# Two layers of each expert as seven block products instead of eight, with streamed weights

## The chip, the cores and the metric

The kernel runs on one core of a Trainium2 chip. The core has five engines with a queue each, worked off in order: TensorE (PE, matmul; its weight loads are shown as PEld), VectorE (DVE), ScalarE (ACT), GpSimd (POOL) and SyncE (SP, which here issues nearly all DMA transfers). They wait for each other by semaphores. The metric is the device time of one execution in microseconds. SBUF is the on-chip memory that all engines read; PSUM is the small one that only PE's products go to, in eight banks of 128 x 512 fp32.

## The reference

Input is `x` of shape (1, 32, 128, 256): 4096 tokens of 256 channels. All arithmetic is fp32. There are two layers.

- Layer 0 normalises the tokens, projects q, k, v, computes masked attention over all 4096 tokens in 8 heads, and adds the projected result to its input.
- Layer 1 adds an attention in a narrow window of 24 tokens, and then a mixture of eight experts in which every expert sees every token. With `x` the normalised tokens and `w` the softmax of the router's scores:

```python
w = jax.nn.softmax(feat @ Wr + br, axis=-1)
h = jnp.einsum('bfd,edh->bfeh', x, W1) + b1
h = jax.nn.relu(_bn(h, g1, be1, m1, v1))
h = jnp.einsum('bfeh,ehk->bfek', h, W2) + b2
h = jax.nn.relu(_bn(h, g2, be2, m2, v2))
y = jnp.einsum('bfeh,ehd->bfed', h, Wo) + bo
return jnp.einsum('bfed,fe->bfd', y, w)
```

The two batch norms are per-channel scales and shifts with stored statistics, so each of the first two layers of an expert is a 256 x 256 matrix product, a scale, a shift and a relu; the last layer is a 256 x 256 product, weighted by `w` and summed over the experts.

## The kernel before

`fast_kernel` has two stages. The first, up to about 749 us, is layer 0's attention; the change touches nothing in it. The second is layer 1. Its 4096 tokens are eight blocks of 512, and each block goes through the eight experts: the list `work` has 64 pairs (block, expert). The tokens stay in SBUF, one tile of 128 x 256 for 128 tokens. For a block, `expert_tokens` normalises and `turn_tokens` transposes them into `xfT` (256 channels as two halves of 128 partitions, by 512 tokens).

`layer` (L1803 on; products on L1810, relu on L1815) computes one of the first two layers for one block and one expert. For each half `m` of the output channels it takes a PSUM bank and makes two matmuls of 512 columns, one for each half `c` of the input channels; then ACT applies scale, shift and relu to the bank in one instruction. `combine` (products on L1829, DVE on L1837) takes the last layer: eight matmuls of 256 columns into two banks of the pool `ps_y`, after which DVE multiplies by the router's weight and adds onto the tokens; after the last expert of a block the tokens are stored (L1842).

All weights of all experts lie in SBUF: `load_expert` (L1499) loads them in 24 transfers of 256 KB, most of them from `load_rest` between 761 and 790 us. PSUM banks are three for the layers (`ps_h`), two for `ps_y`, three for the other work (`ps_x`, taken with `bank`).

The order of work is the order of the program; the framework adds the semaphores and does not reorder. The main loop at the end of `fast_kernel` does, for each pair, the second layer, `insert()`, the first layer of the next pair, `insert()`, the last layer, `insert()`. So there are three job places per pair. `insert` takes up to four jobs from a list whose order, needs and costs (in us of PE) are given: the rest of layer 1 for later blocks, such as `project` (the projection of layer 0), `normalise` and `turn` (L1588, L1599), `key`, `logits` (L1620), `exponentials` (L1647), `turn_weights` (L1658), `apply` (L1669), `route` (L1732), `turn_route` (L1742), `output_biases` (L1778). A job is taken only when its needs were met in an earlier place, and a job with a cost only while the sum spent stays under a line that grows evenly until ten places before the block begins. `normalise` also issues small transfers (16 KB, L1592 and L1594) that carry edge rows to the neighbours.

A side computation (`bound_squares` and what follows it, on POOL, PE and ACT) bounds the scores and decides on a flag whether a general version must run as well; with these inputs it does not.

In the framework, two accesses to the same PSUM bank of one tile are kept in program order, one of them a write; in SBUF the regions themselves are compared.

Of the kernel before, what the change touches and what calls it, by code (L numbers as in the profile page):

```python
# [16 lines left out]
P = 128  # L17
# [806 lines left out]
def fast_kernel(ctx: ExitStack, tc: tile.TileContext, ins: dict, out: bass.AP, narrow):  # L824
# [91 lines left out]
    with ExitStack() as l0:  # L916
# [540 lines left out]
    wf = ctx.enter_context(tc.tile_pool(name="wf", bufs=1))  # L1457
    W = {
        name: wf.tile([P, E, 2, D], F32, name=f"{name}_sb") for name in ("W1", "W2", "Wo")
    }  # L1460
# [16 lines left out]
    spare = {"tags": itertools.cycle("hxyhxyhx")}  # L1477
# [3 lines left out]
    def open_banks():  # L1481
        nonlocal ps_h, ps_y, ps_x
        early.clear()
        scores_ps.close()
        ps_h = ctx.enter_context(tc.tile_pool(name="ps_h", bufs=3, space=PSUM))
        ps_y = ctx.enter_context(tc.tile_pool(name="ps_y", bufs=2, space=PSUM))
        ps_x = ctx.enter_context(tc.tile_pool(name="ps_x", bufs=3, space=PSUM))
# [9 lines left out]
    def load_expert(e):  # L1497
        for name in ("W1", "W2", "Wo"):
            nc.sync.dma_start(  # L1499
                out=W[name][:, e],  # L1500
                in_=ins[f"L1_ffn_{name}"][e].rearrange("(c p) h -> p c h", p=P),
            )
# [16 lines left out]
    load_expert(0)  # L1519

    def load_rest():
        load_expert(1)
        for b in range(TPB + 1, NBLK):
            load_tokens(b, res.tile([P, TPB, D], F32, name=f"tokens{b}"))
            load_expert(b - 3)
        for e in range(NBLK - 3, E):
            load_expert(e)
        for n in range(TPB * TPB, NTILE):
            with_bias(n)
# [195 lines left out]

    def route(b):
# [56 lines left out]
    def layer_halves(src, name, l, b, e, parts=2):  # L1783

        pss = [ps_h.tile([P, BLK], F32, tag="h", name=f"psh{l}_{b}_{e}_{m}") for m in range(2)]
        for part in range(parts):
            cols = slice(part * BLK // parts, (part + 1) * BLK // parts)
            for m in range(2):
                for c in range(2):
                    nc.tensor.matmul(  # L1790
                        pss[m][:, cols], lhsT=W[name][:, e, c, m * P : (m + 1) * P],
                        rhs=src[:, c, cols], start=(c == 0), stop=(c == 1),
                    )
            if part < parts - 1:
                yield
        dst = fh.tile([P, 2, BLK], F32, tag=f"h{l}", name=f"h{l}_{b}_{e}")
        k = l * E + e
        for m in range(2):
            nc.scalar.activation(
                dst[:, m, :], pss[m], AF.Relu,  # L1800
                bias=bshift[:, m, k : k + 1], scale=bscale[:, m, k : k + 1],
            )
        yield dst  # L1803

    def layer(src, name, l, b, e):
        dst = fh.tile([P, 2, BLK], F32, tag=f"h{l}", name=f"h{l}_{b}_{e}")
        for m in range(2):
            ps = ps_h.tile([P, BLK], F32, tag="h", name=f"psh{l}_{b}_{e}_{m}")
            for c in range(2):
                nc.tensor.matmul(  # L1810
                    ps, lhsT=W[name][:, e, c, m * P : (m + 1) * P], rhs=src[:, c, :],
                    start=(c == 0), stop=(c == 1),
                )
            k = l * E + e
            nc.scalar.activation(  # L1815
                dst[:, m, :], ps, AF.Relu,
                bias=bshift[:, m, k : k + 1], scale=bscale[:, m, k : k + 1],
            )
        return dst

    def combine(ht, b, e):
        w = blk[b]["w"]
        dst = out[0].rearrange("n t d -> (n t) d")
        for r2 in range(TPB // 2):
            ps = ps_y.tile([P, 2, D], F32, tag="y", name=f"psy{b}_{e}_{r2}")
            for k in range(2):
                r = 2 * r2 + k
                for c in range(2):
                    nc.tensor.matmul(  # L1829
                        ps[:, k, :], lhsT=ht[:, c, r * P : (r + 1) * P],  # L1830
                        rhs=W["Wo"][:, e, c, :],
                        start=(c == 0), stop=(c == 1),
                    )
            for k in range(2):
                n = b * TPB + 2 * r2 + k
                r = 2 * r2 + k
                nc.vector.scalar_tensor_tensor(  # L1837
                    out=tokens(n), in0=ps[:, k, :], scalar=w[:, r, e : e + 1],
                    in1=tokens(n), op0=ALU.mult, op1=ALU.add,
                )  # L1840
                if e == E - 1:
                    nc.sync.dma_start(out=dst[n * P : (n + 1) * P], in_=tokens(n))  # L1842
# [11 lines left out]
    def bound_squares(name):  # L1854
        squares[name] = small([P, 2, D], f"sq_{name}")
# [184 lines left out]
    a = layer_halves(blk[0]["xfT"], "W1", 0, 0, 0)  # L2040
# [26 lines left out]
    for b in range(1, NBLK):  # L2067
# [33 lines left out]
        for r2 in range(TPB // 2):  # L2101
# [3 lines left out]
            )  # L2105
        job(("route", b), 0.55, lambda b=b: route(b), ("xfT", b, 0), ("xfT", b, 1))
# [9 lines left out]
        if b == 1:  # L2116
            for name in bound_of:
                job(("square", name), 0, lambda name=name: bound_squares(name))
# [18 lines left out]
    work = [(b, e) for b in range(NBLK) for e in range(E)]  # L2137
# [45 lines left out]
    for k, (b, e) in enumerate(work):  # L2183
        ht = layer(a, "W2", 1, b, e)
        insert()
        if k + 1 < len(work):
            nb, ne = work[k + 1]
            a = layer(blk[nb]["xfT"], "W1", 0, nb, ne)
        insert()
        combine(ht, b, e)  # L2190
        insert()
@with_exitstack
# [46 lines left out]
```

## Time and profile before

| | us |
|---|---|
| median of three runs (lowest to highest) | 1597.08 (1594.83 to 1597.59) |
| the profiled execution | 1596.38 |
| its span, first to last instruction | 1594.4 |
| PE busy, whole span | 1535.3 |
| DVE busy | 888.4 |
| ACT busy | 870.7 |
| POOL busy | 106.8 |
| DMA moved | 30.51 MB |

The page of the profile gives for each engine the busy time and its share, then the chain of work that ended last, followed back from the end. A group line reads: source line, engine, operation, what is written and read, shapes, count, then busy time in all and the mean duration of one in ns, then the idle time of that engine ahead of it and what ended most of that. Matmuls are pipelined: the mean duration of one is longer than the distance from one to the next, so distances are taken from start to start in the timeline. A timeline line reads: start, length of the group, engine, line, operation, count, and in brackets the idle time before it. Busy times by stretch have, after the length, busy time and count of PE, PEld, DVE, ACT and POOL, the granted clock of PE as a share of full, the DMA share and GB/s. One fp32 matmul appears as two records, which the prediction calls passes.

The mean granted clock over the span is 0.988; from 850 to 1450 us it is 1.00 and PE is busy for all but 0.2 us.

### The profile page before, as it was taken

The numbers are of one execution on the slowest core, as the hardware profiler recorded it, in microseconds if no ns is written. First come the engines' busy times: TensorE is split into PE (matmuls) and PEld (weight loads), VectorE is DVE, ScalarE is ACT, GpSimd is POOL, SyncE is SP. The second block draws the span as 40 slices with busy tenths as digits, with TensorE's granted clock in tenths as the row PEclk, the third lists the DMA queues.
The fourth block names the chain that finished last, engine by engine and source line by source line (L and its number), as shares of the span: only waits on it lengthen the run. The fifth ranks groups of instructions, "written<-read, shape, count | busy, mean of one in ns | idle before, by whom it ended". The sixth has DMA issues, their size and how long they took to land.

```text
span 1594.4 us, 20904 instructions
## 1 busy us (share of the span) xinstructions
PE 1535.3 (96%) x8171; PEld 710.3 (45%) x8171; DVE 888.4 (56%) x1508; ACT 870.7 (55%) x1156; POOL 106.8 (7%) x295
## 2 busy tenths in 40 slices
PE   8899899999999999998799999999999999999998
PEld 5333232232222222222456565566665666556555
DVE  3666778888898898999533232333332323233211
ACT  3676777878888888986243334334333342434222
POOL 1111002000000000003401000000000000000000
PEclk9999999999999999999799999999999999999999
DMA  4210000000000010000600000000000000000000
GB/s 107 60 29 17 22 8 24 8 21 8 2 8 8 1 47 21 1 8 21 203 4 1 4 14 3 14 1 10 7 4 14 0 4 14 3 14 0 14 0 15
DMA packets 36344, 30.51 MB, mean 19 GB/s; under 512 B 10008, under 2 KB 34319, under 8 KB 36239
## 3 DMA queue, kind: packets, MB, share of 16 engines
q1 hardware_dynamic: 35088, 28.02, 6.2%
q8 instruction: 66, 1.08, 0.3%
q10 hardware_dynamic: 1150, 1.09, 0.3%
q14 instruction: 40, 0.32, 0.1%
HBM read 23.63 MB, written 4.32 MB: 18 GB/s over the span
## 4 chain that ended last, share of the span: by engine, by line
PE 88%; ACT 4%; DVE 2%; DMA 2%; issue 2%; SPq 0%; POOL 0%; ACTq 0%; DVEq 0%; POOLq 0%
PE psh L1810 28%; PE sa L1248 16%; PE av L1292 14%; PE psy L1829 14%; PE psq L983 2%; ACT pt L1262 2%; PE psv L998 2%; PE psk L970 2%; PE psk L1608 2%; PE sb L1248 1%; PE sums L1318 1%; ACT pt L1260 1%; PE pso L1559 1%; PE pss L1620 1%; DVE acc L1282 1%
## 5 line engine op out<-in xcount | busy, mean ns | idle before, releaser
L1282 DVE TENSOR_TENSOR acc<-acc,pt 128x1024 f32<-128x1024 f32 (+3 forms) x500 | 525.2, 1115 | 43.8 <-ACT pt L1262 31.7
L1815 ACT ACTIVATE h<-psh,bshift,bscale 128x512 f32<-128x512 f32 x254 | 197.3, 777 | 416.9 <-PE psh L1810 416.7
L1262 ACT ACTIVATE pt<-sb 128x1536 f32<-128x1536 f32 (+3 forms) x288 | 387.3, 1345 | 3.3 <-PE sb L1248 3.2
L1248 PE MATMUL sa<-q,kT 32*128 32x512 f32 (+3 forms) x576 | 302.2, 604 | 7.3 <-ACT pt L1260 5.3
L1248 PE MATMUL sb<-q,kT 32*128 32x512 f32 (+3 forms) x1728 | 306.1, 604 | 2.2 <-ACT pt L1262 1.1
L1292 PE MATMUL av<-pt,v 128*32 128x512 f32 (+3 forms) x2304 | 286.2, 569 | 2.7 <-POOL pt L1266 1.3
L1837 DVE SCALAR_TENSOR_TENSOR tokens<-psy,w,tokens 128x256 f32<-128x256 f32 x256 | 111.8, 478 | 259.0 <-PE psy L1829 259.0
L1829 PE MATMUL psy<-Wo_sb,h 128*128 128x256 f32 x1024 | 233.3, 381 | 0.4 <-ACT h L1815 0.4
L1810 PE MATMUL psh<-h,W_sb 128*128 128x512 f32 x512 | 231.4, 595 | 0.0
L1810 PE MATMUL psh<-xfT,W_sb 128*128 128x512 f32 x504 | 227.2, 593 | 0.0
L1260 ACT ACTIVATE pt<-sa 128x512 f32<-128x512 f32 (+3 forms) x288 | 162.5, 564 | 95.0 <-PE sb L1248 70.9
L1829 PEld LDWEIGHTS psy<-Wo_sb,h 128*128 128x128 f32 x1024 | 192.1, 190 | 40.1 <-issue 15.6
L1248 PEld LDWEIGHTS sa<-q,kT 32*128 32x128 f32 x576 | 84.2, 182 | 217.5 <-ACT pt L1260 178.1
L1810 PEld LDWEIGHTS psh<-xfT,W_sb 128*128 128x128 f32 x504 | 93.4, 190 | 104.4 <-issue 102.3
L1810 PEld LDWEIGHTS psh<-h,W_sb 128*128 128x128 f32 x512 | 95.2, 190 | 99.9 <-issue 97.6
L1292 PEld LDWEIGHTS av<-pt,v 128*32 128x32 f32 x2304 | 45.4, 108 | 201.8 <-issue 182.8
L1266 POOL MEMSET pt<- 32x128 f32 (+2 forms) x192 | 58.5, 304 | 658.6 <-ACT pt L1262 574.3
L1248 PEld LDWEIGHTS sb<-q,kT 32*128 32x128 f32 x1728 | 88.0, 182 | 9.5 <-ACT pt L1262 6.9
L1282 DVE TENSOR_TENSOR acc<-pt,pt 128x1024 f32<-128x1024 f32 (+1 forms) x32 | 36.7, 1188 | 35.5 <-ACT pt L1262 30.6
L1635 DVE SCALAR_TENSOR_TENSOR s<-pss,negb,bandb 128x144 f32<-128x144 f32 x64 | 16.1, 294 | 47.4 <-PE pss L1620 47.4
L1679 DVE SCALAR_TENSOR_TENSOR tokens<-psa,sum,tokens 128x256 f32<-128x256 f32 x32 | 15.0, 468 | 44.9 <-PE psa L1673 44.9
L1745 POOL MEMSET w<- 128x128 f32 x8 | 1.6, 206 | 533.5 <-DVE tokens L1837 533.5
(227 smaller groups left out, 959.0 us busy)
## 6 DMA issues: line engine op xcount, KB each, us to landing
xg<-in_x_dram SPq DMA_DIRECT2D x32, 128.0 KB
tokens<-in_x_dram SPq DMA_DIRECT2D x8, 512.0 KB
W_sb<-in_L_ffn_W_dram SPq DMA_DIRECT2D x16, 256.0 KB
out_dram<-tokens SPq DMA_DIRECT2D x32, 128.0 KB
rec<-flat SPq DMA_DIRECT2D x60, 64.0 KB
xs<-in_x_dram SPq DMA_DIRECT2D x24, 128.0 KB
Wo_sb<-in_L_ffn_Wo_dram SPq DMA_DIRECT2D x8, 256.0 KB
xh<-xl SPq DMA_DIRECT2D x62, 16.0 KB
```

The source lines that it names most:

```text
L970: nc.tensor.matmul(ps, lhsT=wKT[:, c, g * P : (g + 1) * P], rhs=hT[:, c, :], start=(c == 0), stop=(c == 1),)
L983: nc.tensor.matmul(ps, lhsT=wcT[:, c, g * P : (g + 1) * P], rhs=hT[:, c, :], start=(c == 0), stop=(c == 1),)
L1248: nc.tensor.matmul((sb[:, h - 1, :] if h else sa)[:, lo:], lhsT=kT[rows, g, j * P : (j + 1) * P], rhs=q[rows, g, lo:], start=True, stop=True,)
L1260: nc.scalar.activation(pt[:, 0, lo:], sa[:, lo:], AF.Exp, scale=SCALE)
L1262: nc.scalar.activation(pt[:, 1:, lo:], sb[:, :, lo:], AF.Exp, scale=SCALE)
L1266: nc.gpsimd.memset(pt[k * N : (k + 1) * N, :, lo : lo + k * N], 0.0)
L1282: nc.vector.tensor_tensor(live[b, g][:, hs, lo:], old[:, hs, lo:], pt[:, hs, lo:], op=ALU.add)
L1292: nc.tensor.matmul(av[h * HD : (h + 1) * HD, lo:], lhsT=v[:, j, (g * HG + h) * HD : (g * HG + h + 1) * HD], rhs=pt[:, h, lo:], start=(j == ...
L1810: nc.tensor.matmul(ps, lhsT=W[name][:, e, c, m * P : (m + 1) * P], rhs=src[:, c, :], start=(c == 0), stop=(c == 1),)
L1815: nc.scalar.activation(dst[:, m, :], ps, AF.Relu, bias=bshift[:, m, k : k + 1], scale=bscale[:, m, k : k + 1],)
L1829: nc.tensor.matmul(ps[:, k, :], lhsT=ht[:, c, r * P : (r + 1) * P], rhs=W["Wo"][:, e, c, :], start=(c == 0), stop=(c == 1),)
L1837: nc.vector.scalar_tensor_tensor(out=tokens(n), in0=ps[:, k, :], scalar=w[:, r, e : e + 1], in1=tokens(n), op0=ALU.mult, op1=ALU.add,)
```

## The change

- **Block products.** For experts from the fourth pair on, the 256 x 256 by 256 x 512 product of each of the first two layers is taken as a 2 x 2 by 2 x 2 block product in the Winograd form of Strassen's scheme: seven products of 128 x 128 weights with 256 token columns in place of eight. It needs four sums of weight blocks (`weight_sums`, POOL, once per expert) and four sums of token blocks (`token_sums`, DVE: one operation of 512 and two of 256 columns; once per block for the first layer, in the new job `sums`, and once per pair for the second layer). Of the output, three blocks need sums as well: ACT copies one product to SBUF (`u`), DVE makes three adds of 256 columns and, after the last products, one of 512, and the relu is one ACT instruction of 256 columns from PSUM, one of 256 and one of 512 from SBUF. Some products accumulate onto others in PSUM.
- **Two halves of a layer.** `Layer.first` issues four products, the copy and three adds; `Layer.last` three products, the add of 512 and the relus. Each layer takes two banks of `ps_h`, now four; `ps_x` has two instead of three.
- **Order.** One round of the loop is: first layer of the next pair, first half; `insert`; half of an older combine; second layer of this pair, first half; `insert`; last half of the first layer; another half combine; the token sums of the new hidden tile; last half of the second layer; `insert`. The combine runs 1.5 pairs behind.
- **Streams.** Weights are no longer kept. Each round loads W1 and W2 of the pair two ahead (two transfers of 256 KB) and Wo of this pair (256 KB); from block 1 on it also loads the weight sums (512 KB), which block 0 writes to DRAM after computing them.
- Some squares of the side computation share two tiles, so two of them wait for earlier columns; early banks are cycled in another order.

```diff
-    wf = ctx.enter_context(tc.tile_pool(name="wf", bufs=1))
-    W = {
-        name: wf.tile([P, E, 2, D], F32, name=f"{name}_sb") for name in ("W1", "W2", "Wo")
-    }
+    wf = ctx.enter_context(tc.tile_pool(name="wf", bufs=3))
+    wdr = ctx.enter_context(tc.tile_pool(name="wdr", bufs=1, space=bass.MemoryType.DRAM))
...
-        ps_h = ctx.enter_context(tc.tile_pool(name="ps_h", bufs=3, space=PSUM))
+        ps_h = ctx.enter_context(tc.tile_pool(name="ps_h", bufs=4, space=PSUM))
         ps_y = ctx.enter_context(tc.tile_pool(name="ps_y", bufs=2, space=PSUM))
-        ps_x = ctx.enter_context(tc.tile_pool(name="ps_x", bufs=3, space=PSUM))
+        ps_x = ctx.enter_context(tc.tile_pool(name="ps_x", bufs=2, space=PSUM))
...
+    def load_layers(k):
+        b, e = work[k]
+        w12[k] = wf.tile([P, 2, 2, D], F32, tag="w12", name=f"w12_{k}")
+        for l in range(2):
+            expert_weights(w12[k][:, l], f"W{l + 1}", e)
+        if b:
+            s12[k] = wf.tile([P, 4, 2, P], F32, tag="s12", name=f"s12_{k}")
+            nc.sync.dma_start(out=s12[k], in_=kept_sums[e])
...
+    def weight_sums(e):
+
+        t = s12[e] = wf.tile([P, 4, 2, P], F32, tag="s12", name=f"s12_{e}")
+        a11, a21, a12, a22 = (
+            w12[e][:, :, c, m * P : (m + 1) * P] for c in range(2) for m in range(2)
+        )
+        for k, (p, q, op) in enumerate((
+            (a21, a22, ALU.add), (t[:, 0], a11, ALU.subtract),
+            (a11, a21, ALU.subtract), (a12, t[:, 1], ALU.subtract),
+        )):
+            nc.gpsimd.tensor_tensor(t[:, k], p, q, op=op)
+        kept_sums[e] = wdr.tile([P, 4, 2, P], F32, name=f"kept{e}")
+        nc.sync.dma_start(out=kept_sums[e], in_=t)
...
+    def token_sums(x, tag, name):
+
+        t = fh.tile([P, 4, HB], F32, tag=tag, name=name)
+        nc.vector.tensor_tensor(
+            t[:, 0:2], x[:, :, HB:], x[:, 0, :].rearrange("p (k c) -> p k c", k=2),
+            op=ALU.subtract,
+        )
+        nc.vector.tensor_tensor(t[:, 2], x[:, 1, HB:], t[:, 0], op=ALU.subtract)
+        nc.vector.tensor_tensor(t[:, 3], x[:, 1, :HB], t[:, 2], op=ALU.subtract)
+        return t
...
+            a, q = self.a, self.q = self.bank(0), self.bank(1)
+            self.product(a[:, 0], w[:, 0, :P], x[:, 0, :HB], True)
+            self.product(q[:, 0], s[:, 0], t[:, 0], True)
+            self.product(a[:, 1], s[:, 1], t[:, 2], False)
+            self.product(q[:, 1], s[:, 2], t[:, 1], False)
+            u = self.u = fh.tile([P, HB], F32, tag="u", name=f"u{self.l}_{self.k}", bufs=3)
+            c22 = self.out[:, 1, HB:]
+            nc.scalar.copy(u, a[:, 0])
+            nc.vector.tensor_tensor(u, a[:, 1], u, op=ALU.add)
+            nc.vector.tensor_tensor(c22, q[:, 0], u, op=ALU.add)
+            nc.vector.tensor_tensor(c22, q[:, 1], c22, op=ALU.add)
...
+            self.product(self.a[:, 0], w[:, 1, :P], x[:, 1, :HB], False)
+            self.product(self.q[:, 0], s[:, 3], x[:, 1, HB:], False)
+            self.product(self.q[:, 1], w[:, 1, P:], t[:, 3], False)
+            e = work[self.k][1]
+            relu(out[:, 0, :HB], self.a[:, 0], self.l, e, 0)
+            flat = out.rearrange("p c t -> p (c t)")[:, HB : 3 * HB]
+            nc.vector.tensor_tensor(
+                flat.rearrange("p (k c) -> p k c", k=2), self.q,
+                self.u.unsqueeze(1).to_broadcast([P, 2, HB]), op=ALU.add,
+            )
+            relu(out[:, 0, HB:], out[:, 0, HB:], self.l, e, 0)
+            relu(out[:, 1, :], out[:, 1, :], self.l, e, 1)
...
+        job(("sums", b), 0, lambda b=b: expert_sums(b), ("xfT", b, 0), ("xfT", b, 1))
...
-    for k, (b, e) in enumerate(work):
-        ht = layer(a, "W2", 1, b, e)
+    PLAIN = 3
...
+    for k in range(len(work)):
+        if k + 2 < len(work):
+            load_layers(k + 2)
+        load_last(k)
+        if k + 2 < E:
+            for e in sums_of.get(k, (k + 2,)):
+                weight_sums(e)
+        one = None
+        if k + 1 < len(work):
+            nb = work[k + 1][0]
+            if k + 1 == PLAIN:
+                expert_sums(0)
+            one = Layer(0, k + 1, blk[nb]["xfT"], blk[nb]["t"] if k + 1 >= PLAIN else None)
+            one.first()
         insert()
-        if k + 1 < len(work):
-            nb, ne = work[k + 1]
-            a = layer(blk[nb]["xfT"], "W1", 0, nb, ne)
+        if k >= 2:
+            combine_half()
+        two = Layer(1, k, *h1.pop(k))
+        two.first()
         insert()
-        combine(ht, b, e)
+        if one:
+            one.last()
+        if k >= 1:
+            combine_half()
+        if one:
+            name = f"th{k + 1}"
+            h1[k + 1] = one.out, token_sums(one.out, "th", name) if k + 1 >= PLAIN else None
+        two.last()
+        h2[k] = two.out
         insert()
+    while halves:
+        combine_half()
```

## The prediction

> **What bounds the kernel now.** I read the page's busy times first, then its chain, then busy times by stretch, then the timeline.
>
> ```profile
> PE 1535.3 (96%) x8171; PEld 710.3 (45%) x8171; DVE 888.4 (56%) x1508; ACT 870.7 (55%) x1156; POOL 106.8 (7%) x295
> ...
> PE 88%; ACT 4%; DVE 2%; DMA 2%; issue 2%; SPq 0%; POOL 0%; ACTq 0%; DVEq 0%; POOLq 0%
> ```
>
> TensorE (PE) is the bound, and the chain lies on it. The average hides that the expert stage is bound by it alone; two stretches show that, one block of eight experts with the attention jobs of the next block woven in, and one expert with no jobs left:
>
> ```profile
> 1190.20:1290.26 100.06, 100.06 (x364) 60.39 (x360) 31.70 (x102) 35.80 (x59) 0.51 (x2) 1.00 0.02 7
> ...
> 1508.16:1518.48 10.32, 10.32 (x34) 6.08 (x32) 1.75 (x4) 3.11 (x4) 0.00 (x0) 1.00 0.14 47
> ```
>
> Columns: length, busy PE, weight loads, DVE, ACT, POOL, granted clock, DMA share, GB/s. PE never idles at full clock; DVE and ACT are busy a third of the time. The timeline of such an expert gives the price of a pass (each fp32 matmul is two passes):
>
> ```profile
> 1508.16 3.60 PE L1810 MATMUL psh<-h,W_sb 128*128 128x512 f32 x8
> 1511.59 3.60 PE L1810 MATMUL psh<-xfT,W_sb 128*128 128x512 f32 x8
> 1515.03 3.62 PE L1829 MATMUL psy<-Wo_sb,h 128*128 128x256 f32 x16
> 1518.48 3.60 PE L1810 MATMUL psh<-h,W_sb 128*128 128x512 f32 x8
> ```
>
> From start to start, 16 passes over 512 columns take 6.87 us (0.429 each) and 16 passes over 256 take 3.45 us (0.2156 each). A new set of weights every 256 columns costs nothing extra. The other prices, by shape:
>
> ```profile
> L1571 DVE TENSOR_TENSOR tokens<-pso,tokens 128x256 f32<-128x256 f32 x25 | 10.4, 418 | 34.2 <-PE pso L1559 34.2
> L987 DVE TENSOR_TENSOR q<-psq,rb 128x512 f32<-128x512 f32 x16 | 11.0, 689 | 25.7 <-PE psq L983 25.7
> L1600 ACT COPY big_t<-ptx 128x256 f32<-128x256 f32 x27 | 8.8, 372 | 12.9 <-PE ptx L1599 12.9
> L1724 ACT COPY xfT<-ptf 128x512 f32<-128x512 f32 x16 | 8.7, 587 | 11.9 <-PE ptf L1720 11.8
> L1588 ACT ACTIVATE xl<-tokens,nmr,rstd 128x256 f32<-128x256 f32 x32 | 17.1, 593 | 5.2 <-DVE nmr L1547 5.2
> ```
>
> **The change, part by part.** *Products.* A layer was 8 passes of 0.429 = 3.43 us and becomes 7 products of 2 passes of 0.2156 = 3.02 us: 0.41 to 0.42 less. Experts 0 to 2 of block 0 stay plain, so 61 x 2 = 122 layers gain 50.8 us. This is the whole gain. An expert without jobs falls from 10.32 to 44 x 0.2156 = 9.49 us of PE.
>
> *New work on DVE and ACT.* Each layer adds one ACT copy (0.37), three dependent DVE adds of 256 (0.42 + 0.04 to the next: 1.34), one add of 512 (0.69), and its relu becomes pieces: 256 from PSUM, then 256 and 512 from SBUF (0.52 + 0.81; the 512 is 0.59 plus 0.22, the difference of the two copies). The sums of hidden tokens add 0.69 + 2 x 0.42 + 0.08 = 1.6 of DVE per expert. DVE then has 2 x 2.03 + 1.6 + 2 x 0.86 (combine) = 7.4 us per expert, plus 2.2 of jobs (31.7 per block less the combine's 14.0, by eight): 9.6 of some 11.7. It fits, but these pieces are a circuit, since each queue is in order: copy 0.41, adds 1.34, combine 0.86, adds 1.34, add 0.69, relus 1.41, sums 1.6, add 0.69, relus 1.41 = 9.75 us with hand-overs, 9.5 if the independent ones overlap as they do in the trace (two adds of L1781 take 0.75). Against 9.49 of PE, the ten experts with no jobs lose 0 to 2.6 us; I take 1.
>
> *Where that leaves the job places.* Of the three places per expert, PE reaches the first only 8 passes (1.72 us) after an expert begins. Walking the circuit, DVE ends the previous expert's last add 1.5 to 2.0 us after that beginning, ACT ends its relus at 2.9 to 3.4, and the adds behind the copy end at 4.6 to 5.2. A job in the first place that needs what ACT or DVE made in the third, or that needs a bank which DVE must first read, now waits; queued behind it on PE are the combine and the second layer. Before, these waits were hidden by idle DVE and ACT and by a third bank for jobs (now two). From the planner's order, in each of the three regular blocks (preparing blocks 4, 5 and 6):
> - the routing transpose waits for the copy of the scores, behind the new sums (1.6): 1.1 us (0.6 to 1.6);
> - two turns follow it; the second needs its bank, read after the adds: 1.9 (1.4 to 2.3);
> - logits behind the second bias pair, likewise: 2.0 (1.5 to 2.5);
> - the weight transposes after an exponential that ACT reaches after the relus: 1.6 (1.2 to 1.9);
> - small ones: 0.4 (0 to 1).
>
> That is 7.0 (4.7 to 9.3) a block, 21 in three. The jobs before and after lie differently: about 5 each for those of blocks 2, 3 and 7 (a third bank in the third place 2.5, weights 1.6, the rest 0.9) and 2.5 for the final routing. Sum 38.5 (25 to 52). No row shows these waits, as nothing in the trace loads DVE like this; the ends come from the two circuits, the middle is mine.
>
> *Streams.* Each expert issues four transfers, 1.25 MB (0.75 MB in block 0, which instead writes 0.5 MB of sums for each expert). At 349 GB/s (the rate in 780 to 785 us) that is 3.8 us, and four issues at about 0.5 are 2.0, requested one expert (9.5 us) ahead. Cost nothing, hidden by 3.7 us of slack. On SP's queue they stand behind edge rows that wait for ACT (438 us of such waits before) and stores that wait for DVE; in about seven experts that could eat the slack, 0 to 2 us each. Taken 0, high end 14. The 24 early weight loads shrink to 4; the stretch before the experts is a chain of small steps on DVE, ACT and PE, so I take 0 (between 5 us less, one load's piece in the chain at 788.65, and 3 more).
>
> *POOL.* Four adds of 256 per expert at 0.69 (2.77 for four of L904) are 2.8 us, one or two experts ahead, on an engine that is idle: cost 0. If the score bound's small operations (862.0 to 865.6) stand ahead, 3.6 us late, still inside an expert of 12 us.
>
> *Early jobs and tail.* The first places with three or more banks: 2 (0 to 4). At the end two halves of the last expert's output remain behind its relus, covered by one older half (1.72 of 2.2): 0.5 against 0.44 idle before; with the last round's thinner cover 0.5 more.
>
> Sum: -50.8 + 1 + 38.5 + 2 + 0.5 = -8.8. The profiled execution took 1596.4 (span 1594.4 and 2.0 around it); that gives 1587.6, and since the median of the runs, 1597.1, lies 0.7 above it, **1588**.
>
> *Row and rule.* After PE had idled 2.87 us (to 797.31) and 1.23 more, 8 passes of 256 took 3.57 us in place of 1.72:
>
> ```profile
> 797.31 1.01 PE L1720 MATMUL ptf<-ident,xf 128*128 128x128 f32 x4 [2.87 <-DVE xf L1711]
> 799.56 3.78 PE L1790 MATMUL psh<-xfT,W_sb 128*128 128x256 f32 x8 [1.23 <-ACT xfT L1724]
> ```
>
> So a wait near 3 us costs about 1.8 more. My waits end below that one by one, so the sum holds none. The Trainium skill (TensorE: Matmul & The Clock Gate, "HAM oscillation") speaks against a change that makes PE wait: it puts the drop to half clock at idle gaps over about 3.4 us, in windows that run freely. By it my sum stays as it is, since no wait reaches 3.4; by the row, waits at their upper ends could each cost a slow stretch.
>
> **The rivals.**
> 1. *PE waits longer at the first job place, and it becomes slower.* About 26 waits (four in a regular block, some fourteen in the rest) make up the 38.5. For: they all hang on one lag, ACT's relus ahead of the copy, and no row shows a relu of this kind from SBUF. Against: each long wait lets DVE catch up. It decides from 8.8 / 26 = 0.34 us more lag; at 0.8 it is 26 x 0.8 = 21 us more: **1609**, and 1618 if five of the waits also cost a slow-clock stretch of 1.8.
> 2. *The waits hide.* If the relus and copies run at overlapped rates throughout, the circuit stays below PE's 9.49 and the lag shrinks by about a microsecond: 26 waits lose 0.8 each: 1588 - 21 = **1567**. For: ACT does four L1588 in 2.08. Against: dependent steps don't overlap.
> 3. *Weights come late.* SP's waits eat the slack: +14, **1602**. Against: DMA is busy 0.02 in such blocks.
> 4. *The products don't get cheaper*, because accumulation into a half bank costs more than the combine's passes: there are 122 x 14 = 1708 such passes, so 0.005 us more on each takes the 8.8 us back, and 0.0075 gives **1601**. Against: the combine's passes have the same shape.
>
> **How the numbers follow.** What a measurement of this kernel can tell from no change is about 0.2%, 3.2 us. Likeliest case (1576 to 1600): 0.39, of it 0.30 faster, 0.06 same, 0.03 slower. Rival 1: 0.32, of it 0.28 slower, 0.03 same, 0.01 faster. Rival 2: 0.20, faster. Rival 3: 0.06, 0.05 slower, 0.01 same. Rival 4: 0.03, 0.01 each way and same. Faster 0.52, same 0.11, slower 0.37. The range runs from rival 2 less 3 to rival 1 with part of its slow clock: 1564 to 1615; the likeliest's own is 1576 to 1600.
>
> **What would show it.** Pass spacing 0.2156 in the block products; an expert without jobs at 9.5 to 9.75 us; a regular block with jobs at 100.07 - 8 x 0.83 + 7 = 100.4 us (98 to 103); PE idle of 1 to 2.5 us before turns, logits and weight transposes in the first place, released by DVE or ACT; DVE near 80% busy; no PE wait on a weight transfer. I am wrong if PE is 100% busy in the regular blocks (rival 2), if granted clock falls there (rival 1), or if products wait for DMA (rival 3).

## The result and the profile after

The changed kernel took 1617.9 us (median of four runs, 1616.3 to 1625.1) against 1596.0 us for the kernel before on the same chip: a ratio of 1.0148, 95% interval 1.0113 to 1.0183. It is 1.5% slower. The prediction was 1588 us, 1564 to 1615, so the time lies 3 us above the range and on the other side of no change. The profiled execution took 1616.3 us (span 1614.5).

Engine totals and the chain, from the page of the kernel after:

```profile
PE 1508.5 (93%) x8903; PEld 858.7 (53%) x8903; DVE 1208.6 (75%) x2203; ACT 938.5 (58%) x1398; POOL 129.3 (8%) x327
...
PE 76%; DVE 10%; ACT 8%; issue 3%; DMA 1%; POOL 1%; SPq 0%; DVEq 0%; ACTq 0%; POOLq 0%
```

TensorE is busy for 27 us less than before and the span is 20 us longer. Its share of the chain fell from 88% to 76%, and VectorE and ScalarE have 18% in place of 6%. Busy times by stretch (length, busy PE, weight loads, DVE, ACT, POOL, granted clock, DMA share, GB/s): two regular blocks and an expert without jobs:

```profile
1120.31:1219.65 99.34, 94.47 (x457) 78.63 (x456) 73.24 (x191) 45.34 (x92) 0.20 (x1) 1.00 0.35 113
1219.65:1320.68 101.03, 96.17 (x458) 79.80 (x456) 73.23 (x191) 45.35 (x92) 0.51 (x2) 0.98 0.35 111
1568.11:1577.60 9.49, 9.49 (x45) 8.38 (x44) 6.75 (x16) 4.25 (x8) 0.00 (x0) 1.00 0.46 138
```

The expert without jobs takes 9.49 us, which is 44 passes of 0.2156, and PE never waits in it: there the change does all it says. A regular block takes 99.3 us, or 101.0 with a stretch at a lower clock in it (3.41 us at 0.50, shown in the last section), against 100.06 before. Its TensorE work is 5.6 us shorter (94.47) and it idles 4.8 us, in four waits. The timeline of four such waits, the first two at the end of the first block and the other two in the second, and an equal wait one block later (brackets: idle time ahead of the row and what ended it):

```profile
1206.60 0.33 PE L1771 MATMUL psrt<-ident,lgT 128*128 128x128 f32 x1 [1.01 <-DVE lgT L1766]
...
1207.72 0.44 PE L1625 MATMUL ptx<-ident,xl 128*128 128x128 f32 x2 [0.58 <-ACT big_t L1626]
...
1234.89 0.81 PE L1646 MATMUL pss<-big_t,kt 128*128 128x160 f32 x4 [1.98 <-DVE tokens L1810]
1235.53 3.02 PE L1924 MATMUL psy<-wo,h 128*128 128x256 f32 x8
...
1249.33 0.33 PE L1684 MATMUL psp<-ident,s 128*128 128x128 f32 x1 [1.26 <-ACT s L1673]
...
1335.91 0.81 PE L1646 MATMUL pss<-big_t,kt 128*128 128x160 f32 x4 [1.97 <-DVE tokens L1810]
1336.55 1.89 PE L1924 MATMUL psy<-wo,h 128*128 128x256 f32 x8
```

The eight output passes behind the wait at 1234.89 took 2.81 us from start to start, those at 1336.55 1.73: the same wait brought a low clock once and not the other time (the last section shows what differs).

The largest loss lies earlier, in the first block of experts (805 to 910 us), where jobs prepare the next block. The timeline of all engines there:

```profile
893.07 0.72 POOL L1528 TENSOR_TENSOR s<-w 128x256 f32<-128x256 f32 x1 [11.65 <-DMA w<-in_L_ffn_W_dram]
...
895.23 0.72 POOL L1528 TENSOR_TENSOR s<-w,s 128x256 f32<-128x256 f32 x1
895.89 0.21 POOL L1774 MEMSET w<- 128x128 f32 x1
...
896.13 0.19 DVE L1777 TENSOR_TENSOR w<-psrt,br 128x32 f32<-128x32 f32 x1 [7.32 <-POOL w L1774]
...
897.55 0.40 DVE L1894 TENSOR_TENSOR u<-psh,u 128x256 f32<-128x256 f32 x1
...
898.01 1.04 PE L1867 MATMUL psh<-h,w 128*128 128x256 f32 x2 [3.71 <-DVE u L1894]
...
905.16 2.07 PE L1585 MATMUL pso<-woT,big_t 128*128 128x256 f32 x4 [3.31 <-ACT big_t L1626]
```

The zeroing of a router tile (0.21 us) stands on POOL behind four sums that have waited 11.65 us for streamed weights. SyncE had issued that load only at 888.37, since its queue stood 12.3 us at an edge row that ScalarE had yet to write. VectorE's queue stands behind the zeroing for 7.3 us, with the adds of a block product in it, and TensorE stands behind those.

Account of the profiled spans from the second half of the very first layer (804.86 us before, 803.48 after) to the end: 789.5 and 811.0 us, **+21.5**. In that stretch PE's listed idle time rose from 2.0 to 47.7 us. From 810 us on, granted clock below 0.97 (windows of 5 us) took 15.3 us in the changed kernel and nothing in the kernel before. Each stretch of low clock costs 1.7 us, so these are nine.

### The profile page after: what moved, and what is told of

Read it like the earlier page. It is cut to its first block, busy times and chain, and to the rows that moved or that the text cites. A ratio compares the mean times of both kernels' runs of the same rounds, so it can differ in the third digit from the quotient of the medians.

```text
span 1614.5 us, 23849 instructions
## 1 busy us (share of the span) xinstructions
PE 1508.5 (93%) x8903; PEld 858.7 (53%) x8903; DVE 1208.6 (75%) x2203; ACT 938.5 (58%) x1398; POOL 129.3 (8%) x327
## 4 chain that ended last, share of the span: by engine, by line
PE 76%; DVE 10%; ACT 8%; issue 3%; DMA 1%; POOL 1%; SPq 0%; DVEq 0%; ACTq 0%; POOLq 0%
PE psh L1867 17%; PE sa L1248 16%; PE av L1292 14%; PE psy L1924 12%; ACT h L1852 3%; PE psq L983 2%; ACT pt L1262 2%; PE psv L998 2%; PE psk L970 2%; PE psk L1634 2%; DVE h L1909 1%; PE sb L1248 1%; PE sums L1318 1%; PE pso L1585 1%; PE psh L1872 1%
## 5 line engine op out<-in xcount | busy, mean ns | idle before, releaser
L1852 ACT ACTIVATE h<-h,bshift,bscale 128x256 f32<-128x256 f32 x244 | 159.2, 699 | 199.6 <-DVE h L1909 199.5
L1924 PE MATMUL psy<-wo,h 128*128 128x256 f32 x1024 | 247.7, 386 | 0.0
L1924 PEld LDWEIGHTS psy<-wo,h 128*128 128x128 f32 x1024 | 195.9, 193 | 30.1 <-issue 4.2
L1894 DVE TENSOR_TENSOR u<-psh,u 128x256 f32<-128x256 f32 x122 | 51.2, 420 | 102.3 <-ACT u L1893 102.2
L1852 ACT ACTIVATE h<-psh,bshift,bscale 128x256 f32<-128x256 f32 (+1 forms) x134 | 77.2, 576 | 74.5 <-PE psh L1867 48.6
L1867 PE MATMUL psh<-tx,s 128*128 128x256 f32 x366 | 90.8, 385 | 1.7 <-DVE tx L1842 1.4
L1867 PE MATMUL psh<-th,s 128*128 128x256 f32 x366 | 89.2, 380 | 0.0
L1909 DVE TENSOR_TENSOR h<-psh,u 128x512 f32<-128x512 f32 x122 | 83.0, 680 | 7.0 <-PE psh L1867 6.8
L1867 PE MATMUL psh<-h,w 128*128 128x256 f32 x244 | 73.7, 384 | 3.7 <-DVE u L1894 3.7
L1867 PEld LDWEIGHTS psh<-tx,s 128*128 128x128 f32 x366 | 70.6, 194 | 12.3 <-issue 1.9
```

The source lines that it names most:

```text
L1852: nc.scalar.activation(dst, src, AF.Relu, bias=bshift[:, m, k : k + 1], scale=bscale[:, m, k : k + 1])
L1867: nc.tensor.matmul(ps, lhsT=w, rhs=x, start=start, stop=True, skip_group_check=True)
L1894: nc.vector.tensor_tensor(u, a[:, 1], u, op=ALU.add)
L1909: nc.vector.tensor_tensor(flat.rearrange("p (k c) -> p k c", k=2), self.q, self.u.unsqueeze(1).to_broadcast([P, 2, HB]), op=ALU.add,)
L1924: nc.tensor.matmul(ps[:, i, :], lhsT=ht[:, c, r * P : (r + 1) * P], rhs=wo[k][:, c, :], start=(c == 0), stop=(c == 1),)
```

## The experiments

Every median stands beside the kernel before in the same chip session. "Stage" is the stretch just defined, in the profiled execution: it leaves out what varies ahead of the experts. Idle time and lost clock are those of the stage, the clock up to its last 15 us, where the outputs are stored.

| kernel | us | ratio to before (95%) | stage | against before | PE idle in it | clock lost from 810 |
|---|---|---|---|---|---|---|
| before | 1593 to 1596 | 1 | 789.5 | 0 | 2.0 | 0 |
| after | 1617.9 | 1.0148 (1.0113–1.0183) | 811.0 | +21.5 | 47.7 | 15.3 |
| plain, new order | 1613.9 | 1.0114 (1.0083–1.0145) | 807.8 | +18.3 | 10.4 | 6.8 |
| block products in the last ten experts | 1603.5 | 1.0058 (1.0042–1.0075) | 798.7 | +9.2 | 10.7 | 6.8 |
| before, new bank split | 1603.8 | 1.0065 (1.0039–1.0091) | 797.5 | +8.0 | 7.6 | 0 |
| ... second measurement | 1601.2 | 1.0052 (1.0035–1.0069) | 798.6 | +9.1 | 7.6 | 1.7 |
| plain, equal places | 1604.0 | 1.0069 (1.0046–1.0093) | 799.1 | +9.6 | 8.7 | 0 |
| after, zeroing on VectorE | 1612.2 | 1.0106 (1.0074–1.0138) | 804.1 | +14.6 | 44.3 | 13.6 |
| after, first place later | 1598.7 | 1.0027 (1.0011–1.0043) | 790.9 | +1.4 | 33.9 | 11.9 |
| after, third job bank | 1599.1 | 1.0029 (1.0012–1.0045) | 793.0 | +3.5 | 36.7 | 12.0 |
| after, token sums last | 1596.3 | 1.0024 (1.0012–1.0037) | 789.9 | +0.4 | 31.3 | 11.9 |
| after, equal places | 1588.0 | 0.9971 (0.9954–0.9988) | 783.5 | −6.0 | 28.2 | 13.6 |
| ... and zeroing on VectorE | 1587.0 | 0.9945 (0.9921–0.9969) | 779.7 | −9.8 | 25.7 | 10.2 |
| ... and token sums last | 1577.8 | 0.9900 (0.9879–0.9921) | 769.1 | −20.4 | 20.3 | 6.8 |
| ... and third job bank | 1560.1 | 0.9779 (0.9755–0.9804) | 753.9 | −35.6 | 11.3 | 3.4 |
| ... and first token sums earlier | 1559.7 | 0.9779 (0.9739–0.9820) | 753.3 | −36.2 | 9.9 | 5.1 |

**1. Plain layers in the new order.**

```
-    PLAIN = 3
+    PLAIN = 64
...
-            if k + 1 == PLAIN:
-                expert_sums(0)
```

> The changed kernel with its new order, banks and streams, but every layer in eight plain products; the sums of weights and of a block's tokens are still made, and no longer read. Lag theory (TensorE waits in the first job place, since the block products' extra copies, adds and split relus load VectorE and ScalarE): the products' 51 us come back onto TensorE, and some 50 us of waits with some 15 us of slow clock go; 1598 to 1605 us, idle of TensorE after 806 us below 10 us. Rival (the new order, the two job banks and the streamed weights make the waits by themselves): the waits stay, and the time is 1640 us or more. If waits on SyncE's queue for weights show, a figure between.

Measured: 1613.9 us, a stage of 807.8. Neither theory holds as it was put; two losses add up. The order, the banks and the streams cost 18.3 us without a single block product, 8.4 of it listed idle time and 6.8 slow clock. And only 3.2 us part this stage from that of the changed kernel, so the 50.8 us of saved passes are eaten, with 3.2 more, by 54 us of waits, slow clock and refilling that the products add. Of the 10.4 us of idle time here, 8.1 lie between 805 and 910 us, in waits of up to 1.80; a regular block has only short ones. Two of them, from its timeline:

```profile
1206.21 0.41 PE L1625 MATMUL ptx<-ident,xl 128*128 128x128 f32 x2 [0.23 <-DVE w L1777]
...
1233.22 0.81 PE L1646 MATMUL pss<-big_t,kt 128*128 128x160 f32 x4 [0.51 <-DVE tokens L1810]
```

The block takes 101.07 us where it took 100.06: 0.74 us of listed idle time costs 1.0.

**2. Block products in the ten experts without jobs only.**

```
-    PLAIN = 3
+    PLAIN = 54
...
-            if k + 1 == PLAIN:
-                expert_sums(0)
```

> Block products from expert 54 on only, the ten experts without jobs; all others plain. If the products' gain is real and the lag costs nothing where no jobs stand: 10 x 0.83 = 8.3 us below the kernel with plain layers throughout (20 layers x 0.417), at an expert of 9.49 us. If the circuit of VectorE and ScalarE costs there too: 3 to 6 us below it.

Measured: a stage 9.1 us shorter than with plain layers (10.4 us by the medians), and an expert of 9.49 us with TensorE fully busy. The products' price was right, and their circuit costs nothing where no jobs stand.

**3. The new bank split in the kernel before.** The reading of plain layers with equal places (next) left some 10 us that neither products nor places explain.

```
-    spare = {"tags": itertools.cycle("hxyhxyhx")}
+    spare = {"tags": itertools.cycle("hxyhxyhh")}
...
-        ps_h = ...(name="ps_h", bufs=3, ...)
+        ps_h = ...(name="ps_h", bufs=4, ...)
...
-        ps_x = ...(name="ps_x", bufs=3, ...)
+        ps_x = ...(name="ps_x", bufs=2, ...)
```

> The kernel before, with nothing changed but the split of the banks: four for layers, two for outputs, two for jobs, in place of three, two and three. Bank theory (with equal places and plain layers, the 10 us that are left against the kernel before are the jobs' third bank: waits for the copy and the bias add that empty one, 0.46 and 0.67 us idle and 1.4 us in each block of 100 us): 8 x 1.4 = 11 us above the kernel before, 1602 to 1606 us, a regular block of 101 to 101.5 us. Rival (the streamed weights and their sums cost it): 1593 to 1596 us, a block of 100.1 us.

Measured: 1603.8 us, a block of 101.06 us (1196.60 to 1297.66). The bank theory holds: the new split, which takes one of three banks from the jobs, costs the old kernel about 0.65%, with the same two waits. From its timeline:

```profile
1297.66 0.41 PE L1599 MATMUL ptx<-ident,xl 128*128 128x128 f32 x2 [0.23 <-DVE w L1748]
...
1324.66 0.81 PE L1620 MATMUL pss<-big_t,kt 128*128 128x160 f32 x4 [0.51 <-DVE tokens L1781]
```

**4. Plain layers, job places 3.44 us apart.** In the changed kernel the three places of an expert stand 1.72, 3.44 and 5.16 us of TensorE work apart; here they are equal again (`PLAIN` is 64 as in experiment 1; those lines are left out).

```
             one.first()
-        insert()
         if k >= 2:
             combine_half()
+        insert()
         two = Layer(1, k, *h1.pop(k))
         two.first()
-        insert()
         if one:
             one.last()
+        insert()
```

> Plain layers throughout as in the first run, with the three job places 3.44 us apart as before the change: the first behind the half of an output product that followed it, the second behind the last half of the next expert's first layer. Order theory (unequal places, 1.72, 3.44 and 5.16 us apart, make the 15 us of waits and the slow clock that plain layers had at 1613.9 us): 1595 to 1600 us, TensorE idle after 806 us below 6 us. Rival (the streams, two job banks or the early order make them): 1608 to 1614 us, with the waits of 811 to 905 us as they were.

Measured: 1604.0 us, between the two. Against unequal places the stage is 8.7 us shorter, and 6.8 of that is slow clock that is gone (in part luck, see the last section). The rest against the kernel before is 9.6 us; experiment 3 gives 8.0 of it to the banks. That leaves 1.6 us, by the difference of single traces, for the streamed weights, the sums on POOL and the rest of the order: with plain layers the streams are as good as free.

**5. The changed kernel with its first place 1.72 us later.**

```
             one.first()
-        insert()
         if k >= 2:
             combine_half()
+        insert()
```

> The first job place is moved behind the half of an output product (8 passes, 1.72 us) that stood after it. Lag theory: TensorE reaches the place 1.72 us later, so the waits of a regular block (1.01, 0.58, 1.98, 1.26) fall to at most 0.3 in sum, the block to about 95 us, and some 30 us of the 48 go with most of the slow clock: 1575 to 1590 us. Rival (VectorE at 75 to 80% is the limit whatever the place, so a job that comes later makes another wait): 1605 to 1617 us, with new waits of 1 to 2 us in the second place or before the output products.

Measured: 1598.7 us. The regular block takes 95.5 us, as the lag theory had it, but its waits sum to 1.5 us and not to 0.3 at most. The time misses the theory's 1575 to 1590, since waits elsewhere stayed: near 900 us they are 4.34 and 4.15. The regular block's from the timeline:

```profile
1202.86 0.44 PE L1625 MATMUL ptx<-ident,xl 128*128 128x128 f32 x2 [0.46 <-ACT big_t L1626]
...
1228.76 0.81 PE L1646 MATMUL pss<-big_t,kt 128*128 128x160 f32 x4 [1.03 <-DVE tokens L1810]
```

Both that are left look like waits for a job bank to be emptied; the next experiment tests that.

**6. The changed kernel with a third job bank,** taken from the outputs.

```
-    spare = {"tags": itertools.cycle("hxyhxyhh")}
+    spare = {"tags": itertools.cycle("hxyhxxhh")}
...
-        ps_y = ...(name="ps_y", bufs=2, ...)
+        ps_y = ...(name="ps_y", bufs=1, ...)
-        ps_x = ...(name="ps_x", bufs=2, ...)
+        ps_x = ...(name="ps_x", bufs=3, ...)
```

> The changed kernel as it was, with one bank for outputs and three for jobs instead of two and two. Bank theory (the wrong side of the prediction comes from the jobs' lost bank): of the 4.8 us idle in a regular block the 1.98 before the logits and the 0.58 before the second turn go, 8 blocks x 2.6 = 21 us with the like of them elsewhere, and some slow clock: 1590 to 1598 us. Rival (the waits belong to VectorE's lag at the first place, and each goes to the next thing that is late): 1608 to 1617 us.

Measured: 1599.1 us, 1 us above the bank theory's range, and a block of 96.2. The 0.58 and the 1.98 are gone, the other two unmoved:

```profile
1194.54 0.33 PE L1771 MATMUL psrt<-ident,lgT 128*128 128x128 f32 x1 [1.02 <-DVE lgT L1766]
...
1232.43 0.33 PE L1684 MATMUL psp<-ident,s 128*128 128x128 f32 x1 [1.25 <-ACT s L1673]
```

So these two waits were the bank, and those two the queues. The price of a single output bank shows elsewhere: new waits of 1.02 and 0.97 us in the last output products, and one of 4.17 at 892.73.

**7. The changed kernel with the token sums last.** The sums of hidden tokens wait for ScalarE and take 1.6 us of VectorE ahead of the second layer's last add; here they follow it.

```
+        two.last()
+        h2[k] = two.out
         if one:
             name = f"th{k + 1}"
             h1[k + 1] = one.out, token_sums(one.out, "th", name) if k + 1 >= PLAIN else None
-        two.last()
-        h2[k] = two.out
```

> The changed kernel as it was, with nothing edited but the position of the hidden tokens' sums, behind the second layer's last add (the file of the run before held, by a slip, the old kernel with the new bank split, and not this edit). Lag theory: the 1.01 before the routing transpose and the 1.26 before the weight transposes of a regular block go, the 1.98 shrinks: 1590 to 1602 us. Rival (the sums are only moved, and hold the next layer or the bank's release as long): 1612 to 1622 us.

Measured: 1596.3 us, inside the lag theory's range. It isn't right in every wait. In a regular block:

```profile
1194.70 0.33 PE L1771 MATMUL psrt<-ident,lgT 128*128 128x128 f32 x1 [1.53 <-DVE lgT L1766]
...
1195.71 0.47 PE L1625 MATMUL ptx<-ident,xl 128*128 128x128 f32 x2 [0.46 <-ACT big_t L1626]
...
1223.70 0.81 PE L1646 MATMUL pss<-big_t,kt 128*128 128x160 f32 x4 [0.95 <-DVE tokens L1810]
...
1235.45 0.33 PE L1684 MATMUL psp<-ident,s 128*128 128x128 f32 x1 [0.25 <-ACT s L1673]
```

The weight transposes' wait fell from 1.26 to 0.25 and the logits' from 1.98 to 0.95, but the routing transpose waits 1.53 in place of 1.01: the copy of the scores, last in VectorE's queue in both kernels, comes later, since VectorE now idles 0.42 us ahead of the add (1190.71) with the sums still behind it. Of the two waits near 900 us, the first falls from 3.71 to 2.50 and the second from 3.31 to 1.52. In the changed kernel the second wait's copy stood behind relus (903.54), these behind the last add (902.83), and that behind the token sums (901.30 to 902.91); so these sums were 1.8 us of it.

An earlier run meant for this edit held, by a slip in its file, the kernel of experiment 3. So its expectation was not tested by it:

> The changed kernel as it was, with the sums of the next expert's hidden tokens behind the second layer's last add. Lag theory (the prediction's lag of ScalarE's relus and of the copies behind 1.6 us of sums is what makes the waits at the first place): the adds, the copies of scores and the relus come 1.6 us sooner, the 1.01 before the routing transpose and the 1.26 before the weight transposes of a regular block go, the 1.98 shrinks: 1590 to 1602 us. Rival (the sums are only moved, and hold the next layer's or the bank's release as long): 1612 to 1622 us.

It is a second measurement of the old kernel with the new bank split: 1601.2 us, ratio 1.0052 (1.0035 to 1.0069).

**8. The changed kernel with the router's tile zeroed on VectorE.**

```
-        nc.gpsimd.memset(wide, 0.0)
+        nc.vector.memset(wide, 0.0)
```

> The zeroing of the router's tile on VectorE in place of GpSimd, where it stood behind the sums of streamed weights. Theory (it held VectorE for 7.3 us near 895 us, and so TensorE at 898.01 and 905.16): both waits of 3.7 and 3.3 us go, and with them the slow clock of 895 to 910 us (0.82, 0.84, 0.66 in three windows of 5 us, 3.4 us lost): 1617 - 10 = 1607 us. Rival (what is late behind it takes its place): 1614 to 1617 us. The regular blocks stay at 99.3 to 101 us under both.

Measured: 1612.2 us, a stage 6.9 us shorter, between the theories. One of the two waits went, the other stayed. From the timeline of all engines:

```profile
890.88 0.33 PE L1771 MATMUL psrt<-ident,lgT 128*128 128x128 f32 x1 [1.01 <-DVE lgT L1766]
...
892.62 0.17 DVE L1774 MEMSET w<- 128x128 f32 x1
...
892.89 0.19 DVE L1777 TENSOR_TENSOR w<-psrt,br 128x32 f32<-128x32 f32 x1
...
903.29 1.13 PE L1585 MATMUL pso<-woT,big_t 128*128 128x256 f32 x4 [3.43 <-ACT big_t L1626]
```

VectorE no longer waits for the zeroing, so POOL's queue was the cause of the 3.71. The 3.3 to 3.4 has another, of which experiment 7 shows a part.

**9. The changes together.** Block products with equal places as in experiment 4:

> The changed kernel with its block products and the places 3.44 us apart. Order theory: below the kernel with the first place moved alone (1598.7) by what the second place gains, 1580 to 1592 us; a regular block at 93 to 95 us, its waits below 1.2 us. Rival (VectorE's circuit decides, and a job in the second place now comes right behind the first layer's relus): 1598 to 1608 us, with waits of 1 to 2 us at the second place.

Measured 1588.0 us, in the order theory's range and faster than before (0.9971). Its regular block of 96.0 us misses the 93 to 95, with waits of 0.46, 0.46 and 1.03. Waits of 0.46 at the second place (a key product behind a copy) are new, but small. With the zeroing on VectorE as well:

> The same, and the router's tile zeroed on VectorE. Alone that took 6 us off the changed kernel (1617.9 to 1612.2). If its wait near 897 us is still there with equal places: 5 to 8 us below the kernel with equal places. If equal places already let the sums of weights end in time: 0 to 2 us.

Measured: 3.8 us off the stage, with 2.5 less idle time and 3.4 less slow clock, and intervals of the ratio that overlap, so neither forecast is borne out by time. In the traces the wait was still there with equal places (3.35 at 892.96), and it goes. Then the token sums last:

> The same as the last, and the sums of the next expert's hidden tokens (1.6 us of VectorE, waiting for ScalarE's relus) stand behind the second layer's last add instead of ahead of it. Queue theory (that add, and the relus that follow it, are late because VectorE's queue waits at the sums): the last waits for transposes and weight transposes go, 4 to 10 us below the kernel without it. Rival (the sums are then late themselves, for the second layer of the next expert): no gain, or 2 to 10 us above, with waits of the products on the sums.

Measured 1577.8 us: 10.6 us off the stage, as the queue theory had it and a little more, of it 5.4 idle time and 3.4 slow clock. The waits of a regular block did not go, though: their sum fell from 2.09 to 1.59 (0.46, 0.46 and 0.67 are left). Then three banks for jobs and one for outputs:

> The kernel with equal places, the zeroing on VectorE and the sums last (1577.8 us), with one bank for outputs and three for jobs. Bank theory: the three waits of a regular block (0.46, 0.46, 0.67 us) and those like them go: 8 blocks x 1.6 to 2.0 = 13 to 16 us less, 1562 to 1566 us, a block of 94 us. Rival (the output products now wait for the one bank, which VectorE empties 0.9 us behind them and later where its queue is full): 1575 to 1590 us, with waits at the output products.

Measured 1560.1 us, 2 us below the range; blocks of 94.6 and 94.9, in which one wait of 0.74 took the place of the three. And the first token sums one expert earlier:

> The same, and the sums of the first block's tokens are made one expert earlier. TensorE waited 1.41 us for them near 838 us: 1 to 3 us less than without it (with a slow stretch of the clock where that wait brings one); 0 if another wait stands behind it.

Measured 1559.7 us, not to be told from the last by time; the wait of 1.41 us is gone from the trace. This version's page and two of its regular blocks (columns as above):

```profile
PE 1488.7 (96%) x8903; PEld 849.8 (55%) x8903; DVE 1209.1 (78%) x2211; ACT 943.2 (61%) x1398; POOL 127.8 (8%) x319
...
PE 85%; ACT 6%; DVE 4%; issue 2%; POOL 1%; DMA 1%; ACTq 0%; DVEq 0%; SPq 0%; POOLq 0%
```

```profile
1082.64:1177.20 94.56, 93.82 (x457) 78.60 (x457) 73.38 (x193) 45.97 (x92) 0.31 (x1) 1.00 0.38 119
1177.20:1272.11 94.91, 94.17 (x457) 78.59 (x457) 73.49 (x193) 45.97 (x92) 0.00 (x0) 1.00 0.37 119
```

VectorE does as much as in the changed kernel (1209 us), is busy for a larger share of the block (73.4 of 94.6 us, 78%, in place of 73.2 of 99.3, 74%), and TensorE waits 0.74 us. The load was not the limit. With the same products and the same streams the kernel is 2.2% faster than before (1.8 to 2.6); what changed is where the waiting instructions stand.

## Why the prediction was wrong

Its sum was −8.8 us, and the profiled span rose by 20.1. The steps that failed are two terms put at next to nothing, slow clock at 0 and the early jobs at 2, and one that was not there. Of the 28.9 us between, the trace gives listed idle time 5.2 more than forecast, slow clock 15.3 in place of 0, and −2.9 of small terms (below). The other 11.3 us are what remains. Gaps too short to be listed sum to 0.5 us in the stage, so nearly all of it is time in which PE counts as busy at full clock; that it is the refilling behind each wait is argued from the blocks below, not measured wait by wait.

- *Products, −50.8.* Right. An expert without jobs takes 9.49 us as forecast, and experiment 2 finds 9.1 for ten experts where 8.3 were due. Its circuit was given 1 us and cost none.
- *Regular blocks, 100.4 (98 to 103).* Right: 99.3 and 101.0. Listed waits are 1.01, 0.58, 1.98 and 1.26 against 1.1, 1.9, 2.0 and 1.6, and the small ones of 0.4 are not there. The second turn was overrated. That the block comes out so near is part luck: 4.8 us of listed idle time in place of 7.0, and 1.1 of refilling and 1.7 of slow clock that the sum did not hold.
- *The reasons for those waits.* Half right. The prediction hung them all on one lag. Experiments 5 to 7 show three causes, of which each alone takes 18 to 21 us off the stage: the place that TensorE reaches too early, the lost bank, the sums ahead of an add. They overlap, and each figure holds 3.3 to 3.4 of slow clock. The bank was named, but the 8.0 us that it costs plain layers were never set apart. The prediction counted no banks in use in the old trace.
- *Jobs of blocks 2, 3, 7 and the final routing, 17.5.* 17.9 of listed idle time from 910 us on outside the regular blocks. Right in sum. The longest wait of the trace, 3.82 us at 1006.89 (a turn behind VectorE's L1777), is among them; no single wait was forecast above 2.5.
- *Early jobs 2 (0 to 4), POOL 0.* Wrong. From 805 to 910 us TensorE idles 15.3 us. Of this 7.0 are the two waits behind POOL and ScalarE near 900; experiment 8 shows POOL's queue to be the cause of the first, experiment 7 the token sums to be 1.8 us of the second. The prediction priced POOL's work and asked whether the sums come in time, not who stands behind them in POOL's queue: the zeroing, and behind it all of VectorE. In the sum this was half hidden by regular blocks that idle 14.5 us and not 21.
- *Slow clock, 0: "My waits end below that one by one, so the sum holds none".* Wrong, and the largest single error: nine stretches of 1.7 us, five of them between 805 and 910. The prediction had a row for it (1.8 us behind a wait of 2.87) and took it for a threshold. The Trainium skill (TensorE: Matmul & The Clock Gate, "HAM oscillation") speaks of idle gaps over about 3.4 us. Here a wait of 1.98 brought a stretch and one of 1.97 did not, so the measurement decides: short waits, too, cost clock, if they fall together in time as the last section shows. The section's figure of about 1.67 us is the length of one throttled stretch; here a stretch lasts 3.41 us at a granted clock of 0.50, and the 1.7 us are what it loses.
- *Refilling, not in the sum.* A plain block with 0.74 us of listed idle time was 1.00 longer, one with 1.13 was 1.43 longer. The regular block of the changed kernel holds 1.1 us beyond its listed idle time: 99.34 less 4.83 less the 93.4 that its passes take.
- *Streams, 0 (high 14).* Right as a direct cost: at most 1.6 us with all else of the new order (experiment 4), and TensorE waits for no transfer. But the late load at 888.37, behind an edge row as rival 3 had it, is where the wait of 3.71 begins.
- *Small terms.* Experts begin 1.4 us earlier and the tail and the last circuit cost nothing. The forecast had 1.5 for these two.

Of the rivals the first came nearest (1609, and 1618 with slow stretches): slower by waits at job places, with slow clock on top. It was right by its second clause. Its mechanism, 0.8 us more lag at every wait, was not seen, since the waits of a regular block were shorter than forecast; that its 1618 is the measured time is luck. Rivals 2 and 4 are out: TensorE waits, and a pass costs what it should. Rival 3 is out as put, since no product waits for a transfer, though its late load did occur near 888 us, with POOL and VectorE between it and TensorE.

What stays open: which waits below some 1.95 us bring a slow stretch, what the 11.3 us are wait by wait, and what the other 1.5 us of the second wait near 900 us hang on.

## What to carry to other kernels

When work moves from the bounding engine to others, their busy share says little: the same VectorE load gave 1618 us and 1560 us. Ask of each new instruction what stands behind it in its queue, and of each bank taken from a pool how long its last user keeps it; price both on the old kernel first, by one run with the new bank split and one with the new order and the old arithmetic. Waits of one to two microseconds on TensorE cost more than they show, in refilling and in stretches of low clock.

## What the runs showed of the hardware that was not expected

- A stretch of low clock is 3.41 us at a granted clock of 0.50, and so costs 1.7 us. In the changed kernel the nine stretches (the first at 812.89, the last at 1485.32) begin whole multiples of 3.41 us apart, so time can be counted in the steps of that grid. The step ahead of the stretch at 1236.14 holds the whole wait of 1.98. The wait of 1.97 a block later is cut by the grid into about 1.2 and 0.8, and the clock stays at 1.00. Two steps of each (columns as above):

```profile
1232.73:1236.14 3.41, 1.44 (x9) 1.20 (x8) 2.34 (x7) 0.33 (x2) 0.00 (x0) 1.00 0.63 223
1236.14:1239.56 3.42, 3.42 (x9) 2.72 (x9) 1.46 (x5) 0.00 (x0) 0.00 (x0) 0.50 0.01 3
...
1331.72:1335.13 3.41, 2.21 (x12) 1.35 (x10) 2.31 (x7) 1.56 (x3) 0.00 (x0) 1.00 0.79 250
1335.13:1338.55 3.42, 2.64 (x14) 2.42 (x15) 2.11 (x8) 0.00 (x0) 0.00 (x0) 1.00 0.39 139
```

- In the sixteen traces, from 810 us to the last 15, all 33 steps with at least 1.95 us of listed idle time were followed by one at half clock. Of the full-clock steps with 0.69 to 1.95 us, 27 of 136 were, and of those with less none. Below 1.71 us all that were held narrow products too (weights of 32 rows, or one column), so the listed idle time is not all that counts. So the same waits can cost clock or not, by where the grid lies. The kernel of experiment 3 shows it: in its first measurement waits of 0.51 and 0.19 (825.52 and 826.73) fell into two steps and it lost nothing; in its second they (823.22 and 824.43) fell into one, and this stretch followed:

```profile
825.27:828.69 3.42, 3.42 (x7) 1.61 (x6) 0.99 (x4) 0.01 (x1) 0.00 (x0) 0.50 0.00 0
```

- In two plain blocks, what is lost behind short waits is some 30% more than the trace lists as idle (0.74 listed, 1.00 lost; 1.13 and 1.43).
- 1.25 MB of weights streamed for each expert, 119 GB/s through a whole block with a DMA share of 0.37, left TensorE at full clock and 99% busy (the blocks at the end of experiment 9).
